# Graph convolution over 412,500 edges: six block buffers, scatters from chunk 369 on paced one by one, the second quad of nodes later

## Chip, cores and metric

The kernel runs on one core of one Trainium2 chip. The metric is the device time of one execution in microseconds; each version is timed several times and the median is compared. The engines are named as in the profile: PE is TensorE, DVE VectorE, ACT ScalarE, POOL GpSimd, SP SyncE.

## The reference

A graph convolution with a layer norm ahead of it and a residual around it. 12,500 nodes have 128 features each, 412,500 edges have 20 attributes and a weight each.

```python
h = relu(layernorm(x))                      # 12500 x 128
h = h @ W_in2f
Wij = ssp(f_ij @ W_f1 + b_f1) @ W_f2 + b_f2 # 412500 x 128, ssp(x) = softplus(x) - log 2
Wij = Wij * rcut_ij[:, None]
x_ij = h[idx_j] * Wij
agg = segment_sum(x_ij, idx_i, 12500)
return x + ssp(agg @ W_o1 + b_o1) @ W_o2 + b_o2
```

In the call `idx_i` is `src` and `idx_j` is `dst`; the edges come sorted by `dst`. So the rows `h[idx_j]` of neighbouring edges lie close together, and the sums over `idx_i` go to nodes all over the table.

## The kernel before

**Chunks and segments.** The edges are cut into 806 chunks of 512 (four tiles of 128). The chunks form seven segments; the first has chunks 0 to 351. Each chunk's 512 messages are computed and written, by four indirect DMAs (scatters) of 128 rows each, into slots of a table in HBM that are sorted by blocks of 128 target nodes. When a segment's last chunk is 17 steps back (`DELAY`), its collection begins: the slots of one block after another are read back (`m`), compared with the node numbers (`to`, L932), and added up by TensorE as products with the comparison (L953, into `acc`); `keep` (L987 on DVE for later segments) adds the result to the sums `agg`. So from step 369 (352 + 17) on a step holds a chunk's own work and a piece of collecting, called its units.

**A step.** The program is unrolled, and each engine executes its instructions in the order in which they are written. The function `step(k)` writes: the message of chunk `k` on DVE (`message`: the place L863, and `o = v * hg` L864); the end of the last rank on DVE (`rank_end`: `top` L771); on ACT the scaled rows of chunk `k+1` (`picked`: `hg`, L856); on PE the filters of chunk `k+1` (`value`: `v`, L834); on PE the picks of node rows of chunk `k+2` (`pick`, L846), from rows `near` that SP loaded; on ACT the bias of its `v` (L826); on DVE `at` (`window`, L818), every second step `r` (`hidden_end`, L742), and `inb`, which marks the block of each edge for a later chunk (`blocks`, L747); the comparisons `to` of the units; on PE the ranks of a later chunk (`pass_on` L799 and `rank` L766, which read `inb`), from which `top` and, for every four chunks, the slot numbers are made; every second step on ACT the softplus parts `a` (L719 to L722) and on PE the hidden layer `z` (`hidden`, L710); and last on PE the additions of the units (`add`, L953).

**The scatters.** `message` puts its chunk on the list `waiting`. The four scatters of a chunk (L873, on GpSimd's own DMA queue) read `o`, of which there are 16 buffers. The first 24 chunks scatter as soon as `o` is there. From chunk 24 (`PACED`) on, the scatters of chunk `k-1` (`LAG` is 1) are written right behind PE's `v` of chunk `k+1`, and the first of the four waits for the last matmul of that `v`; the other three follow with no wait for PE. In the last 12 steps nothing is paced. GpSimd does hardly anything else than scatters.

**The head.** The node table is made in quads of 512 nodes by `make_h`, a generator that does one stage at each call: statistics on DVE (L346, L347), normalisation on DVE (L355 to L362), transposition on PE (L367) and `relu` on ACT, the product with `W_in2f` on PE (L373), the split into three bf16 parts on ACT and DVE (L377, L380), and the writes of the table by SP (L386, L395). Quad 0 is made ahead of the loop. Quad 1 (`h[1]`) does its first stage in step 0 and one stage more at the end of each step from 0 on. `HEAD` (steps 0, 2, 4) places the hidden layer's parts in the first steps.

Of the kernel before, what the change touches and what calls it, by code (L numbers as in the profile page):

```python
# [11 lines left out]
F16 = mybir.dt.float16  # L12
# [33 lines left out]
def gnn_kernel(  # L46
# [498 lines left out]
    with tc.tile_pool(name="edge", bufs=2) as edge, tc.tile_pool(  # L545
# [57 lines left out]
        class Group:  # L603
# [101 lines left out]
            def hidden(self, c):  # L705

                z = psum.tile([P, 2, CH], F32, name="z")
                for k in range(2):
# [3 lines left out]
                    if k == 1:  # L712
                        behind(mm, self.g * NCHUNK + c - LZ, 3)
                self.pair[c] = z
# [30 lines left out]
            def blocks(self, c):  # L745
                inb = quad.tile([P, QT, NBLK], F16, name="inb")
# [6 lines left out]
            def rank(self, c):  # L753
# [8 lines left out]
                if k == seg.cleared and k > seg.c0:  # L762
# [3 lines left out]
                nc.tensor.matmul(free, after, self.inb[c], start=k == seg.c0, stop=False,  # L766
                                 skip_group_check=True)
# [61 lines left out]
            def value(self, c, v):  # L829
# [8 lines left out]
                kept["v"] = mm  # L838
                return v

            def pick(self, c, at, ps):
# [3 lines left out]
                for i in range(QT):  # L845
                    mm = nc.tensor.matmul(ps[:, i, :], at[:, i * P:(i + 1) * P], near,  # L846
                                          start=i == 0, stop=i == QT - 1, skip_group_check=True)
                    if i == 1:
                        behind(mm, k, 2 + k % 2)

# [16 lines left out]
            def scatter(self, c, after=None):  # L867

                views = self.seg.views
                o = self.o.pop(c)  # L870
                for i in range(QT):
# [8 lines left out]
                    if i == 0 and after is not None:  # L880
# [13 lines left out]
        class Collect:  # L894
# [47 lines left out]
            def add(self, u):  # L942
                b0, nb, t0, nt = self.units[u]
                m, to = self.m.pop(u), self.to.pop(u)
                for j in range(nb * nt):
# [5 lines left out]
                    if i == 0 and t == 0:  # L951
                        self.acc[b // few] = self.room(b // few)
                    nc.tensor.matmul(self.acc[b // few][:, i, :], m[:, j, :P], to[:, j, :],  # L953
                                     start=t == 0, stop=t == self.seg.tiles(b) - 1)
# [96 lines left out]
        LAG, PACED = 1, 24  # L1051

        def step(k, units=()):
# [12 lines left out]
            def message(k):  # L1066
                g, c = of(k)
                g.message(c, vs.pop(k), hgs.pop(k))
                waiting.append(k)
                scatter(k)  # L1070

            def scatter(k, after=None):
                while waiting and (waiting[0] < PACED or k >= NCH - PACED // 2
                                   or after is not None and waiting[0] <= k - LAG):
                    j = waiting.pop(0)
                    g, c = of(j)
                    g.scatter(c, after if j >= PACED and k < NCH - PACED // 2 else None)
# [3 lines left out]
            if not k:  # L1081
                next(h[1])
# [11 lines left out]
            if has(k + 1):  # L1094
                g, c = of(k + 1)
                hgs[k + 1] = g.picked(c, ps.pop(k + 1))
                if k + 1 not in vs:
                    vs[k + 1] = g.value(c, bs.pop(k + 1))
                    scatter(k, kept["v"])
            if k in HEAD:  # L1100
                part("log", k + LZ - 1, pairs(hidden_log))
            if has(k + 2):
# [3 lines left out]
                g.pick(c, ats.pop(k + 2), ps[k + 2])  # L1106
                if k + 2 > 0:
                    bs[k + 2] = g.bias(c)
            part("window", k + 3, window)
# [9 lines left out]
            if 0 <= k < HEAD[-1]:  # L1119
# [7 lines left out]
            for r in ready[-1:]:  # L1127
                next(r, None)
                tops.append(r)
            if k in HEAD:  # L1130
# [5 lines left out]
            for c, u in units:  # L1136
                if summed:
                    summed[0].add(summed[1])
                summed[:] = c, u

# [131 lines left out]
        with tc.manual_schedule():  # L1272
# [36 lines left out]
            for k in range(-3, max(NCH, max(units) + 1)):  # L1309
# [11 lines left out]
                if k >= 0:  # L1321
                    for m in h:
# [127 lines left out]
```

## Time and profile before

| | us |
|---|---|
| median of 3 runs | 5023.69 |
| their lowest and highest | 5019.35, 5025.19 |
| profiled execution | 5066.41 |
| its span, first to last instruction | 5064.7 |

The mean granted clock of TensorE in the profiled execution is 0.784 of full speed. Over the span PE is busy 71%, DVE 62%, POOL 62%, ACT 55%. Times in the quoted lines are microseconds unless marked ns; a line such as "L873 POOL" is an instruction written at line 873 of the kernel and executed by GpSimd. A group's row gives the number of instructions, their busy time and the mean of one in ns, and the idle time of the engine just before them with what ended most of it. "issue" is a gap in which the engine waited for nothing that the profile shows; "remote" is something that the trace could not name.

### The profile page before, as it was taken

How to read it: one execution, taken by the hardware profiler on the slowest of the kernel's cores; microseconds unless marked ns; L12 is line 12 of the kernel's file. 1: busy time of each engine (PE TensorE's matmuls, PEld its weight loads, DVE VectorE, ACT ScalarE, POOL GpSimd, SP SyncE). 2: the span in 40 equal slices, each digit the busy share in tenths (PEclk: the TensorE clock that was granted, in tenths of full speed). 3: DMA queues.
4: the chain of work that ended last, by engine and by line, in shares of the span. 5: the costliest groups of instructions: out<-in, count | busy, mean ns of one | idle time of the engine just before them, and what ended most of it. 6: DMA issues, size and time to landing. Idle time of an engine off the chain costs nothing. (4 is left out here: it accounts for less than half of the span.)

```text
span 5064.7 us, 68387 instructions
## 1 busy us (share of the span) xinstructions
PE 3601.4 (71%) x21594; PEld 2760.7 (55%) x21594; DVE 3149.0 (62%) x7192; ACT 2793.9 (55%) x5494; POOL 3135.5 (62%) x3298
## 2 busy tenths in 40 slices
PE   5666666566655565567777887887777787787778
PEld 3444444344433344356666666666666666666667
DVE  5565555555544454556666666666666676677767
ACT  5556566565555555555555555555555555555533
POOL 5566666666666666666666666666656666666553
PEclk7666666766666666679999888888988888888889
DMA  4555545445433334446657655567656765665658
GB/s 140 171 160 164 171 138 174 147 134 160 130 99 114 113 113 141 131 154 199 190 189 238 187 178 185 175 192 230 188 169 185 219 207 168 183 216 163 186 144 229
DMA packets 494767, 858.10 MB, mean 169 GB/s; under 512 B 141018, under 2 KB 276558, under 8 KB 494398
## 3 DMA queue, kind: packets, MB, share of 16 engines
q1 hardware_dynamic: 390798, 640.38, 42.3%
q0 software_dynamic: 103168, 213.15, 12.5%
q8 instruction: 174, 2.85, 0.2%
q14 instruction: 195, 1.60, 0.1%
q10 hardware_dynamic: 432, 0.13, 0.0%
HBM read 457.62 MB, written 395.69 MB: 168 GB/s over the span
## 5 line engine op out<-in xcount | busy, mean ns | idle before, releaser
L873 POOL DMA_INDIRECT slots<-o,slot x3224 | 3090.8, 959 | 1831.2 <-issue 808.9
L856 ACT ACTIVATE hg<-picked,rcut 128x128 f32<-128x128 f32 x3224 | 913.3, 366 | 1243.5 <-remote 356.7
L834 PEld LDWEIGHTS v<-wf,r 128*128 128x128 f32 x6448 | 1067.2, 247 | 324.2 <-issue 214.8
L834 PE MATMUL v<-wf,r 128*128 128x128 f32 x6448 | 1153.8, 335 | 73.4 <-issue 36.5
L864 DVE TENSOR_TENSOR o<-v,hg 128x512 f32<-128x512 f32 x806 | 553.0, 686 | 698.4 <-remote 207.0
L953 PEld LDWEIGHTS acc<-to,m 128*128 128x128 f32 x5660 | 782.1, 219 | 281.0 <-issue 144.0
L953 PE MATMUL acc<-to,m 128*128 128x128 f32 x5660 | 836.6, 308 | 117.1 <-DVE agg L987 45.2
L710 PE MATMUL z<-f,wf 20*128 20x512 f32 x1612 | 605.7, 826 | 355.7 <-issue 185.6
L771 DVE TENSOR_REDUCE top<-free 128x4 f32<-128x392 f32 x806 | 449.1, 557 | 602.2 <-remote 341.9
L932 DVE TENSOR_TENSOR to<-numbers,m 128x640 f32<-128x640 f32 (+3 forms) x793 | 630.4, 825 | 40.0 <-remote 12.0
L719 ACT ACTIVATE a<-z,bf 128x1024 f32<-128x1024 f32 x402 | 445.7, 1109 | 379.4 <-PE v L834 113.6
L747 DVE TENSOR_TENSOR inb<-numbers,blk 128x392 f16<-128x392 f32 x806 | 447.7, 556 | 297.3 <-PE picked L846 73.9
L846 PE MATMUL picked<-near,at 126*128 126x128 bf16 x3224 | 393.6, 248 | 330.2 <-issue 193.5
L799 PE MATMUL free<-inb,rest_of 128*128 128x392 f16 x806 | 318.1, 395 | 420.9 <-issue 277.2
L742 DVE SCALAR_TENSOR_TENSOR r<-z,nbf,a 128x1024 f32<-128x1024 f32 x402 | 513.5, 1277 | 127.9 <-ACT a L722 64.0
L826 ACT ACTIVATE v<-bf 128x512 f32<-128x512 f32 x806 | 486.6, 604 | 180.7 <-DVE o L864 72.5
L846 PEld LDWEIGHTS <-at 126*128 126x128 bf16 x3224 | 302.7, 114 | 389.7 <-issue 364.5
L953 PE MATMUL numbers<-to,m 128*128 128x128 f32 x2492 | 398.7, 324 | 121.0 <-DVE to L932 87.6
L953 PEld LDWEIGHTS numbers<-to,m 128*128 128x128 f32 x2492 | 367.5, 233 | 213.6 <-DVE to L932 136.6
L722 ACT ACTIVATE a<-a,half 128x1024 f32<-128x1024 f32 x402 | 461.5, 1148 | 13.1
L710 PEld LDWEIGHTS z<-f,wf 20*128 20x128 f32 x1612 | 152.4, 226 | 551.7 <-issue 303.0
L720 ACT ACTIVATE a<-a 128x1024 f32<-128x1024 f32 x402 | 424.9, 1057 | 12.8
(126 smaller groups left out, 1845.0 us busy)
## 6 DMA issues: line engine op xcount, KB each, us to landing
m<-slots SPq DMA_DIRECT2D x307, 387.0 KB
rel<-rel_d SPq DMA_DIRECT2D x202, 504.0 KB
m<-slots SPq DMA_DIRECT2D x278, 322.5 KB
f<-in_f_t SPq DMA_DIRECT2D x101, 512.0 KB
slots<-o,slot POOLq DMA_INDIRECT x3224
m<-slots SPq DMA_DIRECT2D x193, 258.0 KB
slots<-zero SPq DMA_DIRECT2D x96, 387.0 KB
slots<-zero SPq DMA_DIRECT2D x58, 516.0 KB
```

What stands on the lines that cost most here:

```text
L710: mm = nc.tensor.matmul(z[:, k, :], wf1[rows, :], self.f[rows, :], start=True, stop=True)
L722: nc.scalar.activation(a, a, AF.Ln, bias=half, scale=0.5)
L742: nc.vector.scalar_tensor_tensor(r, z, nbf1, a, op0=ALU.max, op1=ALU.add)
L771: nc.vector.tensor_reduce(self.top[:, c * QT:(c + 1) * QT], free_v, axis=mybir.AxisListType.X, op=ALU.max)
L826: nc.scalar.activation(v, spread(bf12, QT), AF.Copy)
L834: mm = nc.tensor.matmul(v[:, i, :], r[:, i * P:(i + 1) * P], wf2, start=False, stop=True, skip_group_check=True)
L846: mm = nc.tensor.matmul(ps[:, i, :], at[:, i * P:(i + 1) * P], near, start=i == 0, stop=i == QT - 1, skip_group_check=True)
L856: nc.scalar.activation(hg[:, i, :], ps[:, i, :], AF.Copy, scale=self.rcut[:, j:j + 1])
L864: nc.vector.tensor_mul(o[:, :, :P], v, hg)
L873: put = nc.gpsimd.indirect_dma_start(out=views[j % VIEWS], out_offset=bass.IndirectOffsetOnAxis(ap=self.slot[:, j:j + 1], axis=0), in_=o[: ...
L932: nc.vector.tensor_tensor(to[:, :n, :], count_ps[:, None, :].to_broadcast([P, n, P]), m[:, :n, P:].to_broadcast([P, n, P]), op=ALU.is_equal)
L953: nc.tensor.matmul(self.acc[b // few][:, i, :], m[:, j, :P], to[:, j, :], start=t == 0, stop=t == self.seg.tiles(b) - 1)
```

## The change

It has three parts.

- `inb` has six buffers of its own in place of the pool's three.
- From chunk 369 on (`LONE`, the first segment's end plus `DELAY`) the four scatters of chunk `k-1` are written one at a time, at four points of step `k`: behind `v`, behind the picks, behind the rank, and at the end of the step behind its additions or its `z`. Each waits for PE's last matmul so far (`kept["mm"]`). Chunks 24 to 368 go as before.
- Quad 1 does its stages after steps 6 and later in place of steps 0 to 5; in steps 1 and 3 the hidden layer's `z` and the `v` of chunk `k+2` are written right behind the picks, and the message of chunk 5 is written at the end of step 4.

```diff
--- before.py
+++ after.py
@@ -711,6 +711,7 @@
                                           start=True, stop=True)
                     if k == 1:
                         behind(mm, self.g * NCHUNK + c - LZ, 3)
+                kept["mm"] = mm
                 self.pair[c] = z
 
             def hidden_log(self, c):
@@ -743,7 +744,7 @@
                 self.pair[c] = r
 
             def blocks(self, c):
-                inb = quad.tile([P, QT, NBLK], F16, name="inb")
+                inb = quad.tile([P, QT, NBLK], F16, name="inb", bufs=6)
                 nc.vector.tensor_tensor(
                     inb, count_ps[:, None, :NBLK].to_broadcast([P, QT, NBLK]),
                     self.blk[:, c * QT:(c + 1) * QT, None].to_broadcast([P, QT, NBLK]),
@@ -763,8 +764,8 @@
                     used = self.used()
                     self.limit(6 * len(segs), ALU.is_gt, seg.low, used[:, :, :NBLK - 1])
                     self.limit(6 * len(segs) + 1, ALU.is_gt, seg.low_last, used[:, :, NBLK - 1:])
-                nc.tensor.matmul(free, after, self.inb[c], start=k == seg.c0, stop=False,
-                                 skip_group_check=True)
+                kept["mm"] = nc.tensor.matmul(free, after, self.inb[c], start=k == seg.c0,
+                                              stop=False, skip_group_check=True)
                 kept["inb"] = self.inb[c]
 
             def rank_end(self, c):
@@ -835,7 +836,7 @@
                                           start=False, stop=True, skip_group_check=True)
                     if i == 1:
                         behind(mm, k, k % 2)
-                kept["v"] = mm
+                kept["mm"] = mm
                 return v
 
             def pick(self, c, at, ps):
@@ -847,6 +848,7 @@
                                           start=i == 0, stop=i == QT - 1, skip_group_check=True)
                     if i == 1:
                         behind(mm, k, 2 + k % 2)
+                kept["mm"] = mm
 
             def picked(self, c, ps):
 
@@ -864,11 +866,11 @@
                 nc.vector.tensor_mul(o[:, :, :P], v, hg)
                 self.o[c] = o
 
-            def scatter(self, c, after=None):
+            def scatter(self, c, tiles, after=None):
 
                 views = self.seg.views
-                o = self.o.pop(c)
-                for i in range(QT):
+                o = self.o[c] if tiles[-1] < QT - 1 else self.o.pop(c)
+                for i in tiles:
                     j = c * QT + i
                     put = nc.gpsimd.indirect_dma_start(
                         out=views[j % VIEWS],
@@ -877,7 +879,7 @@
                         in_offset=None,
                     )
                     puts.append(put.ins.name)
-                    if i == 0 and after is not None:
+                    if i == tiles[0] and after is not None:
                         tc.add_manual_dep(
                             put.ins, after.ins.name,
                             mybir.DependencyInfo(mybir.DependencyClass.Sync,
@@ -950,8 +952,9 @@
                     i = b % few
                     if i == 0 and t == 0:
                         self.acc[b // few] = self.room(b // few)
-                    nc.tensor.matmul(self.acc[b // few][:, i, :], m[:, j, :P], to[:, j, :],
-                                     start=t == 0, stop=t == self.seg.tiles(b) - 1)
+                    kept["mm"] = nc.tensor.matmul(
+                        self.acc[b // few][:, i, :], m[:, j, :P], to[:, j, :],
+                        start=t == 0, stop=t == self.seg.tiles(b) - 1)
                     if t == self.seg.tiles(b) - 1 and (i == few - 1 or b == NBLK - 1):
                         self.done.append((b, few))
                         owed.append(self)
@@ -1049,6 +1052,7 @@
         tops, ps = [], {}
         waiting = []
         LAG, PACED = 1, 24
+        LONE = segs[0].c1 + DELAY
 
         def step(k, units=()):
 
@@ -1066,20 +1070,34 @@
             def message(k):
                 g, c = of(k)
                 g.message(c, vs.pop(k), hgs.pop(k))
-                waiting.append(k)
+                waiting.append((k, 0))
                 scatter(k)
 
-            def scatter(k, after=None):
-                while waiting and (waiting[0] < PACED or k >= NCH - PACED // 2
-                                   or after is not None and waiting[0] <= k - LAG):
-                    j = waiting.pop(0)
-                    g, c = of(j)
-                    g.scatter(c, after if j >= PACED and k < NCH - PACED // 2 else None)
+            def scatter(k, point=None):
+                while waiting:
+                    j, i = waiting[0]
+                    if j < PACED or k >= NCH - PACED // 2:
+                        n, after = QT - i, None
+                    else:
+                        where, n = ("v", QT) if j < LONE else ("each", 1)
+                        if point not in (("v", "pick", "rank", "end") if where == "each" else (where,)):
+                            return
+                        if j * QT + i + n > (k - LAG + 1) * QT:
+                            return
+                        after = kept["mm"]
+                    while n > 0:
+                        j, i = waiting.pop(0)
+                        g, c = of(j)
+                        e = min(QT, i + n)
+                        g.scatter(c, range(i, e), after)
+                        after = None
+                        n -= e - i
+                    if e < QT:
+                        waiting.insert(0, (j, e))
+                        return
 
             if k in vs:
                 message(k)
-            if not k:
-                next(h[1])
             for r in tops:
                 for _ in r:
                     pass
@@ -1096,7 +1114,7 @@
                 hgs[k + 1] = g.picked(c, ps.pop(k + 1))
                 if k + 1 not in vs:
                     vs[k + 1] = g.value(c, bs.pop(k + 1))
-                    scatter(k, kept["v"])
+                    scatter(k, "v")
             if k in HEAD:
                 part("log", k + LZ - 1, pairs(hidden_log))
             if has(k + 2):
@@ -1104,8 +1122,12 @@
                 if k + 2 not in ps:
                     ps[k + 2] = psum.tile([P, QT, P], F32, name="picked", tag="v", bufs=3)
                 g.pick(c, ats.pop(k + 2), ps[k + 2])
+                scatter(k, "pick")
                 if k + 2 > 0:
                     bs[k + 2] = g.bias(c)
+                if k in (1, 3):
+                    part("hidden", k + LZ, pairs(hidden))
+                    vs[k + 2] = g.value(c, bs.pop(k + 2))
             part("window", k + 3, window)
             if k not in HEAD:
                 part("end", min(k + LZ - 2, made.get("log", -1)), pairs(hidden_end))
@@ -1116,7 +1138,7 @@
                     keep()
             if k < NCH:
                 keep()
-            if 0 <= k < HEAD[-1]:
+            if 0 <= k <= HEAD[-1]:
                 message(k + 1)
             upto = max(made["rank"], min(k + LR, 2 * k + 3))
             ready = [ranks(j) for j in range(made["rank"] + 1, upto + 1)]
@@ -1127,6 +1149,7 @@
             for r in ready[-1:]:
                 next(r, None)
                 tops.append(r)
+            scatter(k, "rank")
             if k in HEAD:
                 part("end", made["log"] - 1, pairs(hidden_end))
             elif k != -1:
@@ -1137,6 +1160,7 @@
                 if summed:
                     summed[0].add(summed[1])
                 summed[:] = c, u
+            scatter(k, "end")
 
         zeros = {}
         units = {}
@@ -1319,7 +1343,7 @@
                 step(k, now)
 
                 if k >= 0:
-                    for m in h:
+                    for m in h[:1] if k <= HEAD[-1] + 1 else h:
                         next(m, None)
                 if k > NEXT - 3:
                     next(aside, None)
```

**GpSimd**, scatters of two chunks in the second half of the program (`slots1` is the second segment's table, `o` a chunk's messages; DMASW are the scatters' own queue lanes, and the number behind a name in the wait is a count that is left open). Before:

```order
L873 DMA slots1_117<-o_19231,slot_18948 116992x129 [waits DMASW0_49,DVE_49,PE_49]
L873 DMA slots1_117<-o_19231,slot_18948 116992x129 [waits DMASW1_49]
L873 DMA slots1_117<-o_19231,slot_18948 116992x129 [waits DMASW2_49]
L873 DMA slots1_117<-o_19231,slot_18948 116992x129 [waits DMASW3_49]
L873 DMA slots1_117<-o_19284,slot_18948 116992x129 [waits DMASW4_49,DVE_49,PE_49]
L873 DMA slots1_117<-o_19284,slot_18948 116992x129 [waits DMASW5_49]
L873 DMA slots1_117<-o_19284,slot_18948 116992x129 [waits DMASW6_49]
L873 DMA slots1_117<-o_19284,slot_18948 116992x129 [waits DMASW7_49]
```

After, the same scatters:

```order
L875 DMA slots1_117<-o_19231,slot_18946 116992x129 [waits DMASW0_49,DVE_49,PE_49]
L875 DMA slots1_117<-o_19231,slot_18946 116992x129 [waits DMASW1_49,PE_49]
L875 DMA slots1_117<-o_19231,slot_18946 116992x129 [waits DMASW2_49,PE_49]
L875 DMA slots1_117<-o_19231,slot_18946 116992x129 [waits DMASW3_49,PE_49]
L875 DMA slots1_117<-o_19284,slot_18946 116992x129 [waits DMASW4_49,DVE_49,PE_49]
L875 DMA slots1_117<-o_19284,slot_18946 116992x129 [waits DMASW5_49,PE_49]
L875 DMA slots1_117<-o_19284,slot_18946 116992x129 [waits DMASW6_49,PE_49]
L875 DMA slots1_117<-o_19284,slot_18946 116992x129 [waits DMASW7_49,PE_49]
```

The scatters stand in the same order. The second, third and fourth of each chunk now wait for PE too.

**PE in the head**, from the picks of chunk 3 to those of chunk 4 (`z` the hidden layer, `xps` the transposition of quad 1, `v_461` before and `v_438` after the filters of chunk 3). Before:

```order
L846 MATMUL picked_456<-near_285,at_405 128x128
L799 LDWEIGHTS rest_of_78
L799 MATMUL free_144<-inb_409,rest_of_78 128x392
L766 LDWEIGHTS after_77
L766 MATMUL free_144<-inb_465,after_77 128x392
L799 LDWEIGHTS rest_of_78
L799 MATMUL free_144<-inb_465,rest_of_78 128x392
L766 LDWEIGHTS after_77
L766 MATMUL free_144<-inb_467,after_77 128x392
L710 MATMUL z_483<-f_227,wf1_62 128x512 x2
L367 MATMUL xps_486<-ident_58,xb_236 128x128 x4
L834 MATMUL v_461<-wf2_63,r_426 128x128 x4
```

After:

```order
L847 MATMUL picked_433<-near_285,at_392 128x128
L710 MATMUL z_440<-f_227,wf1_62 128x512 x2
L835 MATMUL v_438<-wf2_63,r_413 128x128 x4
L800 LDWEIGHTS rest_of_78
L800 MATMUL free_144<-inb_396,rest_of_78 128x392
L767 LDWEIGHTS after_77
L767 MATMUL free_144<-inb_449,after_77 128x392
L800 LDWEIGHTS rest_of_78
L800 MATMUL free_144<-inb_449,rest_of_78 128x392
L767 LDWEIGHTS after_77
L767 MATMUL free_144<-inb_451,after_77 128x392
L847 LDWEIGHTS at_447
```

`z` and `v` of chunk 3 now stand right behind the picks of chunk 3, ahead of four rank products, and quad 1's transposition is gone from between them.

**SP in the head**: `h3_1` to `h3_3` and `h3` are the node tables, `near` the loads of node rows from them. Before:

```order
L629 DMA rel_592<-rel_d_114 126x2048
L386 DMA h3_1_89<-hb_543 128x3x384
L386 DMA h3_2_90<-hb_543 128x4x384
L386 DMA h3_3_91<-hb_543 128x2x384
L395 DMA h3_87<-hb_543 128x4x384
L649 TENSOR_LOAD shift0_130
L656 ISA
L656 DMA near_692<-h3_1_89 126x128
L656 ISA
L656 DMA near_694<-h3_1_89 126x128
```

After, from the third of those loads on:

```order
L629 DMA rel_752<-rel_d_114 126x2048
L656 ISA
L656 DMA near_754<-h3_1_89 126x128
L1335 DMA slots0_116<-zero_82 96x1032 x2
L656 ISA
L656 DMA near_841<-h3_1_89 126x128
L386 DMA h3_1_89<-hb_838 128x3x384
L386 DMA h3_2_90<-hb_838 128x4x384
L386 DMA h3_3_91<-hb_838 128x2x384
L395 DMA h3_87<-hb_838 128x4x384
```

The four writes of quad 1, which stood ahead of four loads from `h3_1`, stand behind them; those loads read rows of quad 0 alone.

## The prediction

> **What bounds the kernel now.** I read the page first, for the engine that is busy longest on work that can't be shared out; then the windows before and after the collection of segments begins, for the time of one chunk in each; then the waits of GpSimd; then a timeline inside the part that the change touches.
>
> ```profile
> span 5064.7 us, 68387 instructions
> PE 3601.4 (71%) x21594; PEld 2760.7 (55%) x21594; DVE 3149.0 (62%) x7192; ACT 2793.9 (55%) x5494; POOL 3135.5 (62%) x3298
> L873 POOL DMA_INDIRECT slots<-o,slot x3224 | 3090.8, 959 | 1831.2 <-issue 808.9
> ```
>
> No engine is full. GpSimd is 62% busy, but each of its 3224 scatters also leaves a fixed gap (808.9 us called "issue"), so that its floor is higher than its busy time tells. Counting the `o` of DVE (L864, one for each chunk) in three windows from the start gives the pace (window, its length, busy time of those instructions and their count, granted clock, share of the DMA engines, GB/s):
>
> ```profile
> 0.00:200.00 200.00, 19.88 (x29) 0.71 0.49 151
> 0.00:2200.00 2200.00, 252.88 (x368) 0.66 0.46 142
> 0.00:4800.00 4800.00, 541.37 (x789) 0.78 0.54 168
> ```
>
> From 200 to 2200 us 368 - 29 = 339 chunks pass, 5.90 us each. From 2200 to 4800 us, which begins almost exactly at chunk 369, it is 789 - 368 = 421 chunks, 2600/421 = 6.18 us each. The second part has TensorE's additions (L953) in every step, and it is the part that the change paces anew. GpSimd there (start, duration, and in brackets the idle time before it and what ended it):
>
> ```profile
> 3603.28 0.95 POOL L873 DMA_INDIRECT slots<-o,slot  x1 [1.84 <-PE z L710]
> ...
> 3607.07 0.96 POOL L873 DMA_INDIRECT slots<-o,slot  x1 [0.30 <-issue]
> 3609.26 0.95 POOL L873 DMA_INDIRECT slots<-o,slot  x1 [1.24 <-PE acc L953]
> ...
> 3618.10 0.96 POOL L873 DMA_INDIRECT slots<-o,slot  x1 [0.30 <-issue]
> 3621.30 0.96 POOL L873 DMA_INDIRECT slots<-o,slot  x1 [2.25 <-PE free L766]
> ...
> 3625.09 0.95 POOL L873 DMA_INDIRECT slots<-o,slot  x1 [0.30 <-issue]
> 3627.38 0.95 POOL L873 DMA_INDIRECT slots<-o,slot  x1 [1.34 <-PE free L766]
> ...
> 3633.41 0.96 POOL L873 DMA_INDIRECT slots<-o,slot  x1 [1.29 <-PE acc L953]
> ```
>
> Inside a run the scatters follow each other by (3618.10 - 3609.26)/7 = 1.263 us, so four cost at least 5.05 us. This window holds runs of 4, 8, 4 and 4, each followed by a stop of 1.24 to 2.25 us; five chunks take 30.13 us, 6.03 each. What the stop waits for is seen on the other engines in the same window:
>
> ```profile
> 3608.72 1.06 PE L834 MATMUL v<-wf,r 128*128 128x128 f32 x8
> 3613.49 2.27 PE L953 MATMUL acc<-to,m 128*128 128x128 f32 x18
> 3619.30 0.22 PE L846 MATMUL picked<-near,at 126*128 126x128 bf16 x1 [1.20 <-issue]
> 3616.48 1.14 ACT L856 ACTIVATE hg<-picked,rcut 128x128 f32<-128x128 f32 x4 [5.62 <-PE acc L953]
> 3617.19 0.57 DVE L771 TENSOR_REDUCE top<-free 128x4 f32<-128x392 f32 x1 [2.34 <-PE v L834]
> ```
>
> During the run of 8 (to 3619.06) TensorE does its work, but ACT stands 5.62 us and DVE 2.34 us for results of TensorE, and then TensorE itself does its picks one by one, 1.2 us apart. An earlier place shows it in the extreme:
>
> ```profile
> 1008.46 0.96 POOL L873 DMA_INDIRECT slots<-o,slot  x1 [0.30 <-issue]
> 1011.21 1.14 ACT L856 ACTIVATE hg<-picked,rcut 128x128 f32<-128x128 f32 x4 [9.66 <-remote]
> 1012.35 0.96 POOL L873 DMA_INDIRECT slots<-o,slot  x1 [2.93 <-remote]
> ```
>
> ACT waits 9.66 us, and its wait ends only 1.8 us after the run's last scatter does (1009.42). I read this so: while scatters follow each other without a stop, news of TensorE's progress reaches the other engines late, and it gets through after GpSimd stops. The kernel is bound by this loop, 5.05 us of scatters and then a stop until the news is through, not by an engine's work.
>
> **The new pace of the scatters, from chunk 369 on.** It holds to chunk 792 (later chunks go unpaced, before and after), 424 chunks. No scatter is added or moved among the scatters; the first of four keeps its wait for `v`; the second, third and fourth wait for the picks, the rank and the last matmul of that same step. That is three more waits for each chunk, 1272. The waiting itself costs GpSimd an instruction each:
>
> ```profile
> L873 POOL DMA_INDIRECT slots<-o,slot x3224: 952/958/1177, 23.2 to 4924.9; - x190
> L873 POOLq EVENT_SEMAPHORE  x832: 17/43/8809, 30.1 to 4912.1; - x167
> ```
>
> With a median of 43 ns (the three numbers are least, median, most) it fits in the 0.30 us between two scatters, so I take 0 (if it did not, 1272 x 43 ns = 55 us, the upper bound). Behind a waiting scatter on GpSimd stands only the next scatter; who waits for scatters is the collection seventeen chunks later, and `o`'s buffers, sixteen chunks deep, so neither is near. What decides is whether the wait is open when a scatter comes to it. In the window above, the fourth scatter of the second chunk of the run of 8 starts at 3618.10, and the last addition of its step ends at 3615.76, 2.3 us before: by the records open. But the stops show that the news may come later than the records, and so some of the fourth scatters will stop.
>
> What does a stop in a new place cost? The stop after a run of 8 is 2.25 us, less the 0.30 that would be there anyway 1.95 for two chunks; those after runs of 4 are 1.24, 1.34 and 1.29, less 0.30 about 1.0 for one. So the price goes with the length of the run, some 0.25 us a scatter. If that holds for shorter runs too, a stop before the fourth scatter shortens the next one by as much, and the move costs nothing; that is the value I take. The other bound is a stop that costs 1.24 - 0.30 = 0.94 however short the run: 424 x 0.94 = 400 us if every chunk had one more. I take the first because two lengths of run show it and none shows the second.
>
> And what can be won? The mean chunk takes 6.18 us, the undisturbed ones above 6.03. The difference, 0.15 x 424 = 64 us, is in long irregular waits (GpSimd's, in total, times, longest):
>
> ```profile
> POOL slots L873 <- PE free L766: 162.1, 84, 2.8
> POOL slots L873 <- PE picked L846: 112.9, 43, 5.5
> POOL slots L873 <- PE z L710: 47.4, 36, 2.2
> ```
>
> From 2400 to 4400 us, 43 waits that end on a pick take 2.63 us each, up to 5.5, twice the 1.32 of those that end on `z`: 43 x 1.31 = 56 us, and over the 2620 us of 424 chunks 74. They come when a run has gone on so long that the picks themselves are late, as at 3619.30. With a wait in each quarter GpSimd can no longer be eight scatters ahead on one piece of news, and what it stops for is nearer, so ACT, DVE and the picks get theirs before the next chunk's first scatter. Some of these stops, those after a run of 8 at 2.25, pay for two chunks and are no loss. So I take 0.11 of the 0.15 us: 424 x 0.11 = 47 us off, between 0 and 74.
>
> The Trainium skill (Perfetto Trace Analysis, "Summary: the profiler window per engine type") says that the end recorded for a TensorE instruction is an estimate and that the travel of its semaphore is hidden. By that rule the 2.3 us of lead above need not be a lead; the trace agrees where ACT waits 5.62 us. It leaves the sum at -47 if stops only move, and turns it into the slower rival below if they add up.
>
> **Six buffers for the blocks.** In the order of instructions DVE's L747 loses only waits on DVE itself; its 155 waits on PE are the same, as they come from the PSUM tile it reads. The row that could bear a buffer's wait is this one, of what L747 idled for:
>
> ```profile
>   PE free L766: 64.2, 18
> ```
>
> If all 18 were the reader of an old block it would be 64 us of DVE, which does not bound; but they are of the late kind above. Gain taken 0, bounds -64 and 0; the buffers themselves add no instruction.
>
> **The second quad of nodes later.** The normalisation, transposition, product and four stores of quad 1 leave the steps 0 to 5 and come after step 6; two pairs of `z` and `v` move up behind the picks.
>
> ```profile
> 35.60 0.96 POOL L873 DMA_INDIRECT slots<-o,slot  x1 [2.38 <-DVE o L864]
> 42.50 0.96 POOL L873 DMA_INDIRECT slots<-o,slot  x1 [2.16 <-DVE o L864]
> 49.23 0.95 POOL L873 DMA_INDIRECT slots<-o,slot  x1 [1.99 <-DVE o L864]
> 57.83 0.96 POOL L873 DMA_INDIRECT slots<-o,slot  x1 [3.86 <-DVE o L864]
> 41.53 0.69 DVE L864 TENSOR_TENSOR o<-v,hg 128x512 f32<-128x512 f32 x1 [2.98 <-PE v L834]
> 38.60 1.12 PE L367 MATMUL xps<-ident,xb 128*128 128x128 f32 x4
> 39.51 1.91 PE L834 MATMUL v<-wf,r 128*128 128x128 f32 x8
> ```
>
> Here alone GpSimd waits for `o`: 10.39 us in four waits, 9.2 beyond the regular 0.30. One of them waits on `v`, which stood behind quad 1's transposition of 1.12 us; that alone is 1 us, all four 9.2. After the move the same work falls where GpSimd has chunks in stock, and SP's four stores stand behind four loads of nodes that read quad 0 only. If they were late for the loads behind them, the 1.12 us and its like come back once: I bound the loss by the same 9.2, and take the middle of the gain, -5.
>
> **Sum.** 5064.7 - 47 + 0 - 5 = 5012.7 us of span. The profiled execution took 5066.41 us, 1.7 beyond its span, and 42.7 more than the median of the runs, 5023.69. So 5012.7 + 1.7 - 42.7 = **4972 us**, 1.0% less.
>
> **Rivals.** *Stops add up (slower).* The place is the fourth scatter: it waits for the additions, which end the step, and `v` of the next step follows directly, so GpSimd may stop twice in a chunk. If each stop has a price of its own, 0.94 us, the 47 us are eaten when more than 47/0.94 = 50 of the 424 chunks have an extra stop, 1 in 8. With 1 in 3 it is 141 x 0.94 = 133 us, less 52: 5105 us. For it speaks how late ACT hears of TensorE; against it that the price of a stop went with the run's length.
>
> *Nothing moves.* All waits are open when GpSimd comes to them, so the change does not pace at all there; runs of 8 stay, and only the head's 5 us remain: 5019 us. For it speaks the lead of 2.3 us; against it the late picks.
>
> *Runs of 8 disappear and the news is in time.* Then the step falls to the pace that the first part reaches with the same scatters, 5.90 us: 424 x 0.28 = 119 us, with the head 4900 us. TensorE would allow it:
>
> ```profile
> 2200.00:4800.00 2600.00, 2053.72 (x13834) 1672.31 (x13834) 1775.36 (x3761) 1414.72 (x2786) 1613.67 (x1685) 0.87 0.62 191
> ```
>
> it is busy 2053.72/421 = 4.88 us a chunk, DVE 4.22. Against it: the two parts differ in additions and in the clock, and a faster pace needs stops shorter than any in the timeline.
>
> **Chances.** The forecast 0.45; stops add up 0.27; nothing moves 0.13; the larger gain 0.15. Two runs of this kernel can be told apart from about 0.2%, 10 us. Faster: the forecast except its weakest edge, and the larger gain, 0.59; same: nothing moves and that edge, 0.14; slower: 0.27. The forecast's own range is 4942 (-74 and -9) to 5020 (no gain but 4 of the head). To leave out no more than 2 in 10 I go down to 4895, just beyond the larger gain, and up to 5095, which takes in extra stops in up to about 3 chunks of 10.
>
> **What would show it.** Right: from 2200 to 4800 us about 428 chunks (2600/6.07); in the timeline stops before the fourth scatter, and the stop before the first one shorter by as much; waits that end on picks down from 43 and none of 5 us; ACT's waits for `hg` below 5 us; scatters still near 958 ns. For the head: the first 60 us without waits for `o` of 2 us and more. Wrong: more than one stop in most chunks with a sum over 1.13 us (6.18 - 5.05), or the same runs of 4 and 8 as before. If the L766 waits of L747 go but the pace stays, the buffers were worth nothing; if the time falls with the scatters' pattern unchanged, they were worth what I gave to the pace.

## The result and the profile after

The changed kernel takes 5000.72 us in the median of 5 runs (4992.46 to 5005.22), the kernel before 5023.69 us (5019.35 to 5032.8) beside it: a ratio of 0.9952, 95% interval 0.9937 to 0.9967. The forecast was 4972 us, 52 us less than before; the runs show 23 less. The direction is right, the size less than half.

In the profile of the changed kernel, the page's row of the scatters and the count of `o` from 2200 to 4800 us (window, length, busy time and count, clock, DMA share, GB/s):

```profile
span 4990.7 us, 69636 instructions
L875 POOL DMA_INDIRECT slots<-o,slot x3224 | 3101.1, 962 | 1740.1 <-issue 772.5
2200.00:4800.00 2600.00, 293.07 (x427) 0.88 0.64 194
```

427 chunks in place of 421, almost the 428 forecast. That agreement is luck, and this is the trap of this case: the two profiles differ by 74 us of span where the medians differ by 23. Chunks 30 to 368, which the pace does not touch, also passed faster, at 5.84 us each in place of 5.90. The profile of before (5066.41 us) lay 43 us above its median, and in three later jobs (each a set of kernels timed together on one chip) the kernel before had medians of 5066.62, 5070.75 and 5073.23 us. So one job's profile can't be held against another's for 1%, and what follows compares kernels of one job, by ratios to the kernel before in that same job.

In three more jobs the kernel before took 4202 to 4209 us in place of 5024 to 5073, on one and the same chip 4209 in one job and 5073 in the next, and nothing in between was seen; what differs in the traces is told with the experiments.

### The profile page after: what moved, and what is told of

Read it like the earlier page. It is cut to its first block, busy times and chain, and to the rows that moved or that the text cites. A ratio compares the mean times of both kernels' runs of the same rounds, so it can differ in the third digit from the quotient of the medians.

```text
span 4990.7 us, 69636 instructions
## 1 busy us (share of the span) xinstructions
PE 3578.4 (72%) x21594; PEld 2746.7 (55%) x21594; DVE 3151.6 (63%) x7192; ACT 2788.5 (56%) x5494; POOL 3145.9 (63%) x3298
## 5 line engine op out<-in xcount | busy, mean ns | idle before, releaser
L875 POOL DMA_INDIRECT slots<-o,slot x3224 | 3101.1, 962 | 1740.1 <-issue 772.5
L955 PEld LDWEIGHTS acc<-to,m 128*128 128x128 f32 x5660 | 778.4, 218 | 280.2 <-issue 171.7
L955 PE MATMUL acc<-to,m 128*128 128x128 f32 x5660 | 831.2, 307 | 119.5 <-issue 56.8
L934 DVE TENSOR_TENSOR to<-numbers,m 128x640 f32<-128x640 f32 (+3 forms) x793 | 630.3, 825 | 35.7 <-remote 16.5
L955 PE MATMUL numbers<-to,m 128*128 128x128 f32 x2492 | 397.2, 324 | 125.8 <-DVE to L934 65.4
L955 PEld LDWEIGHTS numbers<-to,m 128*128 128x128 f32 x2492 | 367.4, 233 | 213.6 <-DVE to L934 110.1
```

What stands on the lines that cost most here:

```text
L875: put = nc.gpsimd.indirect_dma_start(out=views[j % VIEWS], out_offset=bass.IndirectOffsetOnAxis(ap=self.slot[:, j:j + 1], axis=0), in_=o[: ...
L934: nc.vector.tensor_tensor(to[:, :n, :], count_ps[:, None, :].to_broadcast([P, n, P]), m[:, :n, P:].to_broadcast([P, n, P]), op=ALU.is_equal)
L955: kept["mm"] = nc.tensor.matmul(self.acc[b // few][:, i, :], m[:, j, :P], to[:, j, :], start=t == 0, stop=t == self.seg.tiles(b) - 1)
```

## The experiments

**Each part alone, and the kernel before again.** Four kernels of one job. The pace without the buffers and the head:

```diff
-                inb = quad.tile([P, QT, NBLK], F16, name="inb", bufs=6)
+                inb = quad.tile([P, QT, NBLK], F16, name="inb")
...
-                if k in (1, 3):
-                    part("hidden", k + LZ, pairs(hidden))
-                    vs[k + 2] = g.value(c, bs.pop(k + 2))
...
-                    for m in h[:1] if k <= HEAD[-1] + 1 else h:
+                    for m in h:
```

> The kernel before with the new pace of the scatters alone (three block buffers, quad 1 in its old place). The whole change took 23 us off the median (5023.69 to 5000.72). Theory A, the pace is what gains: 4998 to 5008 us, and from chunk 369 to 792 the profile shows about 6.06 us a chunk, as in the changed kernel. Theory B, the pace is worth nothing and the gain lies in the head and the buffers: 5018 to 5028 us, with a chunk at the pace of the kernel before. Theory C, the pace costs and the rest hides it: over 5030 us.

Measured 0.9957 (0.9942 to 0.9972). Theory A: the pace alone carries the change. (Its times of 4998 to 5008 us do not apply, as the kernel before took 5066.62 us in this job, and its 6.06 us a chunk did not come: by the starts of the scatters a chunk from 369 to 792 takes 6.14 us, where the kernel before of this job has 6.16.) The head alone, the same lines of the change put into the kernel before:

> The kernel before with quad 1 moved later alone. As predicted, 5 us off: 5014 to 5021 us, chunk 30 scattered 5 to 10 us earlier than in the kernel before. Rival from the two profiles, where the four waits of 10.4 us in the head became two of 9.2: nothing off, 5020 to 5028 us. Rival that the head carries the change: under 5010 us.

Measured 1.0001 (0.9988 to 1.0015): nothing. In its timeline of GpSimd, what is left of the four waits for `o` in the head:

```profile
44.59 0.96 POOL L873 DMA_INDIRECT slots<-o,slot  x1 [6.36 <-DVE o L864]
57.48 0.96 POOL L873 DMA_INDIRECT slots<-o,slot  x1 [3.00 <-DVE o L864]
```

Two waits of 9.36 us together in place of four of 10.39. The scatters of chunk 2 start 2.2 us sooner (33.5 us in place of 35.7 in this job's kernel before), and then GpSimd is out of messages for longer; chunk 30 starts at 215.2 us, not earlier than the 213.3 of the kernel before. The buffers alone:

```diff
-                inb = quad.tile([P, QT, NBLK], F16, name="inb")
+                inb = quad.tile([P, QT, NBLK], F16, name="inb", bufs=6)
```

> The kernel before with six buffers for the blocks alone. As predicted nothing: 5019 to 5028 us and the same runs of scatters. Rival: the profile of the changed kernel also gained 20 us between chunks 30 and 368, where the pace is unchanged; if the buffers did that, 5000 to 5010 us and an earlier chunk 368.

Measured 1.0011 (0.9997 to 1.0025): nothing. The control:

> The kernel before, word for word, for a second profile and as a measure of the noise. Its first profiled execution took 5066 us, 43 above the median. If that lay in the execution: a profile near 5024 us, and the time from chunk 30 to 368 within 10 us of the changed kernel's 1972 us. If the profile itself costs 40 us: near 5066 again. Ratio 1.000 within 0.002.

Measured 0.9993 (0.9978 to 1.0008), a profile of 5047.22 us where this job's runs of the kernel before had a median of 5066.62 (5050.94 to 5083.19). So the profile does not cost 40 us; single executions spread, and the jobs differ. From chunk 30 to 368 it took 1989 us, 17 more than the changed kernel's 1972 and not within 10: what the changed kernel's profile gained there belongs to its job and not to the change.

Within this job the two profiles may be compared stretch by stretch; not by their spans, which are single executions (5045.5 us, and 5054.2 for the pace alone, the other way than the medians). First the count of `o` from 2200 to 4800 us, of the kernel before (first row) and in the next fence of the pace alone:

```profile
2200.00:4800.00 2600.00, 288.96 (x421) 0.88 0.63 193
```

```profile
2200.00:4800.00 2600.00, 291.64 (x424) 0.88 0.63 193
```

Three chunks more. Then the waits of GpSimd from 2400 to 4400 us (total, times, longest), the kernel before:

```profile
POOL slots L873 <- PE free L766: 140.6, 70, 2.9
POOL slots L873 <- PE picked L846: 105.1, 42, 6.2
POOL slots L873 <- remote: 75.6, 44, 2.7
POOL slots L873 <- PE z L710: 49.1, 35, 2.2
POOL slots L873 <- PE acc L953: 17.0, 13, 2.0
...
POOL slots L873 <- PE numbers L953: 9.2, 7, 1.3
```

and the pace alone:

```profile
POOL slots L875 <- PE acc L955: 109.3, 80, 7.6
POOL slots L875 <- remote: 79.4, 61, 2.2
POOL slots L875 <- PE numbers L955: 59.3, 42, 6.5
POOL slots L875 <- PE free L767: 57.6, 47, 2.6
POOL slots L875 <- PE z L710: 48.6, 41, 2.0
POOL slots L875 <- PE picked L847: 47.5, 35, 2.2
```

The waits that end on the rank and the picks fall from 245.7 to 105.1 us, as forecast, and the long ones on a pick are gone (6.2 to 2.2). But 142.4 us more (109.3 + 59.3 - 17.0 - 9.2) now end on the additions, L953 before and L955 here, and among them are waits of 7.6 and 6.5 us. So this view, which sorts waits by the name of what ended them, does not tell what was won: a wait that leaves one row can stand in another. The names are uncertain too, since in these jobs the traces hold only part of the semaphore updates from which they are inferred (3458 of TensorE's 4063 in this kernel before, 3004 of DVE's 6529). In the timeline of the pace alone GpSimd makes runs of 3, 4, 4, 5 and 4 there:

```profile
3599.81 0.96 POOL L875 DMA_INDIRECT slots<-o,slot  x1 [1.02 <-PE acc L955]
...
3604.60 0.96 POOL L875 DMA_INDIRECT slots<-o,slot  x1 [1.30 <-remote]
...
3610.65 0.96 POOL L875 DMA_INDIRECT slots<-o,slot  x1 [1.30 <-PE acc L955]
...
3616.73 0.96 POOL L875 DMA_INDIRECT slots<-o,slot  x1 [1.32 <-PE free L767]
...
3624.27 0.96 POOL L875 DMA_INDIRECT slots<-o,slot  x1 [1.52 <-remote]
...
3630.31 0.96 POOL L875 DMA_INDIRECT slots<-o,slot  x1 [1.29 <-PE acc L955]
```

From the starts of all scatters of the chunks 369 to 792 in the traces comes this table: ahead of which scatter of a chunk GpSimd stops (a distance of over 1.45 us from the scatter before), in what share of the chunks, and how much that is over 1.265 us, as a mean over all chunks (the control and the pace alone, of one job; then, told of below, the fourth scatter alone at the end of the step, two orders without that end, and the four points from chunk 24 on, of a second job; and the short fill, of a third):

```
                 1st          2nd          3rd          4th         stops   us in all
before_again  0.69 1.10    0.00 0.00    0.00 0.00    0.00 0.00       293     467
pace_only     0.30 0.32    0.10 0.09    0.01 0.01    0.44 0.65       361     451
fourth_at_end 0.27 0.29    0.00 0.00    0.00 0.00    0.51 0.79       328     451
no_end        0.68 1.05    0.06 0.05    0.00 0.00    0.00 0.00       312     465
two_and_two   0.69 1.08    0.00 0.00    0.04 0.04    0.00 0.00       307     472
each_from_24  0.28 0.29    0.08 0.07    0.01 0.01    0.49 0.71       363     456
pad_each_3    0.60 0.88    0.01 0.09    0.02 0.09    0.01 0.09       269     361
```

With a quarter more stops (293 to 361) the stopped time falls by 16 us of 467. (In the last row the four means of 0.09 and a part of 0.88 are the fills told of below.)

Two things move against each other in this sum. All lengths of stops here are what goes over the 1.265 us. In the kernel before (control) a stop lasts 1.02 us in the median after a run of four scatters and 1.87 after a run of eight. In the pace alone it lasts 0.89 after a run of one, 1.27 after two, 0.83 after three, 1.01 after four and 1.82 after eight; runs shorter than four, of which there were none, are now 78 of the 361. Take each stop at the median for its length as the usual part, and what it lasts beyond as the irregular part. In the three kernels of this job with the old pace (head, buffers, control) the usual part is 407 to 410 us and the irregular part 57 to 61; in the pace alone they are 431 and 20. The irregular part falls by 37 to 41 us, the usual part rises by 21 to 25. Stops of over 2.5 us fall from 19 to 22 (71 to 81 us) to 5 (30 us), but the longest, of 8.3 us, is no shorter than the 7.8 of the control.

**Which of the four points does it.** The function that lets scatters go, with a point for each of the four in a list:

```diff
-                        where, n = ("v", QT) if j < LONE else ("each", 1)
-                        if point not in (("v", "pick", "rank", "end") if where == "each" else (where,)):
+                        at = ("v",) * QT if j < LONE else POINTS
+                        if point != at[i]:
                             return
+                        n = at[i:].count(at[i])
...
+        POINTS = ("v", "v", "v", "end")
```

> The kernel before with a new pace in which, from chunk 369 on, the first three scatters of a chunk go behind v as before and only the fourth waits, for the end of the step. With all four points the ratio was 0.9957. Theory A, the fourth scatter's wait is the only one that closes often (in that run a stop of more than 0.2 us stood before 44% of the fourth scatters, 10% of the second, 1% of the third), so it carries the change: 0.994 to 0.997. Theory B, each quarter counts: 0.997 to 1.000.

Measured 0.9965 (0.9952 to 0.9978), and the table's row is close to that of all four points: theory A. With `POINTS = ("v", "pick", "rank", "rank")`:

> The same with the fourth scatter let go with the third, at the rank: points v, picks, rank, rank. Theory A: without the wait for the end of the step the stops stay before the first scatter, and the ratio is 0.999 to 1.001. Theory B: the picks and the rank do part of it, 0.996 to 0.999.

Measured 1.0001 (0.9986 to 1.0017), again A. With `POINTS = ("v", "v", "rank", "rank")`:

> The same with the first two scatters at v and the last two at the rank. Theory A: as without the end, 0.999 to 1.001. Theory B: halves of a chunk give half of the gain or more, 0.996 to 0.998.

Measured 0.9994 (0.9982 to 1.0006), A. The picks and the rank are mostly open when a scatter comes to them (the table has stops before 4 to 10% of the scatters that wait there); only the end of the step closes often. And with the four points of the change from chunk 24 on (`LONE = PACED`):

> The quarters from chunk 24 on, where GpSimd now makes runs of 12. If the idle time only goes with the number of scatters, wherever the stops are, the first part keeps its 5.90 us a chunk and the ratio is that of the change, 0.994 to 0.998. If each stop has a price of its own, one stop more in every chunk of 344 at some 0.5 us costs 170 us: 1.02 to 1.05.

Measured 0.9950 (0.9936 to 0.9964): the idle time does not rise with the stops. In chunks 30 to 368 it made 197 stops where the kernel before of the other job had 147, and 274.9 us in all where that had 279.7 (the other three kernels of its own job, with the old pace there: 150 to 153 stops, 283 to 294 us). More stops do not add up here, and the first part neither gains nor loses more than the noise.

**Fills in GpSimd's time.** If the stopped time is time in which TensorE's news has to get through, it should take other work of GpSimd for nothing. Into the kernel before, behind each scatter of chunks 369 to 792 (a spare tile, so the output is the same):

```diff
                     puts.append(put.ins.name)
+                    if 369 <= self.g * NCHUNK + c <= 792:
+                        nc.gpsimd.memset(pad, 0.0)
```

and, in another, two longer fills behind the fourth scatter alone. The first try of both, with two kernels on the places:

> The same with one short fill (128 x 128 floats, 0.20 us where the trace has one) behind each of the four scatters, so that the 1.07 us of idle time a chunk would be spread over four gaps. Theory N: the news trickles through in the gaps and the stop shrinks by their sum, 0.99 to 1.01. Theory B: 424 x 4 x 0.2 = 340 us more, 1.05 to 1.08.

> The kernel before with two fills of a spare tile on GpSimd (128 x 512 floats each, about 1.06 us together by the fill of 128 x 1032 that took 0.96 us) behind the fourth scatter of each chunk from 369 to 792; nothing else is changed. Theory N, a stop is the time in which TensorE's news get through, and it gets through whenever no scatter is being made: the fills lie in the stop, which shrinks by as much, and the time is nearly the same, ratio 0.995 to 1.02. Theory B, GpSimd's own work sets the pace and the stop comes on top: 424 x 1.06 = 450 us more, 1.07 to 1.10.

> The kernel before with all four scatters of a chunk, from 369 on, at the end of the step in place of v. The fourth scatter alone at the end gave 0.9965. Theory P, the place matters (the stop then lies where TensorE starts on v and the picks): 0.994 to 0.998. Theory S, it is the split of the chunk that breaks the runs of 8: with one stop a chunk again nothing is gained, 0.999 to 1.003.

> The changed kernel with the quarters from chunk 24 on. The pace alone gave 0.9957 from chunk 369 and 0.9950 from chunk 24, so if the parts add up 0.994 to 0.997, no better than the change beyond the noise. A version that beats both would be under 0.993.

Measured 1.0344 (1.0329 to 1.0360), 1.1078 (1.1061 to 1.1094), 1.0002 (0.9993 to 1.0011) and 0.9996 (0.9987 to 1.0005), beside a kernel before of 4202.1 us. This tests none of the theories: in this job GpSimd does not stop at all from chunk 369 to 792, so that fills cost their full price, 0.344 us a chunk for the short ones, and no wait for TensorE has anything to close. The second try, with the change itself:

> The short fill behind each scatter once more (0.344 us a chunk on the chip without stops). If this chip has the stops (kernel before near 5060 us): Theory N, the news gets through whenever no scatter is being made, so the fills come out of the stops, 0.99 to 1.01; Theory B, stop and fills add up, 424 x 0.344 = 146 us, 1.025 to 1.035. On a chip without stops (before near 4200 us): 1.034 again.

> The two fills behind the fourth scatter once more (1.07 us a chunk on the chip without stops). With stops: Theory N 0.995 to 1.02, Theory B 424 x 1.07 = 454 us, 1.08 to 1.10. Without stops: 1.108 again.

> All four scatters at the end of the step once more. With stops: Theory P, the end of the step is the better place for the one stop, 0.994 to 0.998; Theory S, only the split of the chunk gains, 0.999 to 1.003. Without stops: 1.000.

> The changed kernel, word for word. With stops: 0.994 to 0.997, as in its first comparison. Without stops: 0.999 to 1.001, since GpSimd makes scatters without a break there and no wait closes; this says whether the gain belongs to the chip.

Measured 1.0345 (1.0331 to 1.0359), 1.1076 (1.1060 to 1.1091), 0.9998 (0.9989 to 1.0007) and 0.9993 (0.9984 to 1.0002), beside 4208.88 us: without stops again, and there the change is worth nothing. Its profile, the scatters' row and the timeline of GpSimd:

```profile
L875 POOL DMA_INDIRECT slots<-o,slot x3224 | 3103.3, 963 | 1005.2 <-issue 572.4
```

```profile
2999.26 0.96 POOL L875 DMA_INDIRECT slots<-o,slot  x1 [0.30 <-PE picked L847]
3000.53 0.96 POOL L875 DMA_INDIRECT slots<-o,slot  x1 [0.30 <-PE numbers L955]
...
3011.92 0.96 POOL L875 DMA_INDIRECT slots<-o,slot  x1 [0.30 <-issue]
```

A scatter takes what it took, 963 ns, and the distance is 1.266 us ((3011.92 - 2999.26)/10); but the idle time is 1005.2 us, 0.31 a scatter, where it was 1740.1, and ACT's longest wait for `hg` in that stretch is 1.58 us. So the news that comes late in the other jobs is in time here, with the same program. (The names behind the arrows say little here; all waits are the regular 0.30.)

The short fill once more, now in a job with stops, on the chip of the second:

> The short fill behind each scatter a third time, for a chip with stops (before near 5060 us): Theory N 0.99 to 1.01, Theory B 1.025 to 1.035. Without stops 1.034, as twice before.

Measured 1.0014 (0.9996 to 1.0032) beside 5073.23 us, in place of the 1.0345 that the fills cost without stops: theory N. GpSimd in it:

```profile
3601.29 0.96 POOL L874 DMA_INDIRECT slots<-o,slot  x1 [0.16 <-issue]
3602.24 0.22 POOL L882 MEMSET pad<- 128x128 f32 x1
...
3603.98 0.96 POOL L874 DMA_INDIRECT slots<-o,slot  x1 [0.16 <-issue]
3604.94 0.22 POOL L882 MEMSET pad<- 128x128 f32 x1
3606.61 0.96 POOL L874 DMA_INDIRECT slots<-o,slot  x1 [1.45 <-remote]
```

Of the 146 us that the fills cost without stops 7 remain by the ratio, between none and 16. In the traces a stop after a run of 8 falls from 2.01 us in the mean (over the regular distance, control) to 1.42 here, by 0.59 where two chunks' fills are 0.69; the control is of another job.

**Is the news late, or TensorE itself?** The traces hold the times at which semaphores were updated, so the two can be held against each other. In the control, chunks 369 to 792, GpSimd's stops are 21% of the time, and 21% of the TensorE instructions that update its semaphore end in them. But 60% of the updates recorded (1262 of 2090) fall in them, over four a stop, where one would end it. For DVE it is 10% of the ends and 11% of the updates, for ACT 14 and 18%. The records are not complete (2090 updates for 2369 such instructions, and under half for DVE and ACT); if all that are missing for TensorE lay outside the stops, its share would still be 53%. So TensorE's work ends at all times alike, and by the records its news comes mainly while GpSimd stops.

**Place or split.** What all four scatters at the end of the step give where the stops occur, the two jobs without stops could not tell. Once more:

> All four scatters at the end of the step a third time. Where the stops occur (before near 5060 us): Theory P, the end of the step is the better place for the one stop, 0.994 to 0.998; Theory S, only the split of the chunk gains, 0.999 to 1.003. Without stops (before near 4200 us) 1.000, as twice before.

Measured 0.9997 (0.9988 to 1.0006) beside 4202.18 us, without stops a third time. Whether the 0.4% comes from the end of the step as a place, or from splitting the chunk into three and one, stays open.

## Why the prediction came out as it did

- **What bounds the kernel**: right for the jobs with stops. A chunk costs four scatters, 5.06 us, and about 1.1 us in which the news gets through; the fills, which cost 146 us without stops and 7 with them (0.0014 of 5073), show that this time goes to no work of GpSimd. That it is no engine's work the jobs without stops show: 5.06 us a chunk, with the same program. That TensorE's news comes late, which I had read from a few waits, the recorded updates bear out (60% of them in 21% of the time).
- **The stop's price: here the step failed.** I put it at nothing: a stop before the fourth scatter "shortens the next one by as much", at 0.25 us a scatter, measured on runs of four and eight. For shorter runs this does not hold: after one, two and three scatters a stop lasts 0.89, 1.27 and 0.83 us, not 0.25 to 0.75. So the usual part of the stops rose by 21 to 25 us, on a term that stood at 0. The other bound, 0.94 us however short the run, is near for these short runs; it did not make the kernel slower because it was not paid on top: the stops after runs of eight fell from 128 to 22.
- **What is won**, 47 us: the irregular part of the stops fell by 37 to 41 us, near it, and the 64 us that I gave the whole of it is near its 57 to 61; the upper bound of 74 was too wide. What I gave as the reason came only in part. The long waits that ended on picks vanished (6.2 to 2.2 us), but waits of 7.6 us ended on the additions, and ACT did not get its news sooner: from chunk 369 to 792 its waits of over 5 us for `hg`, of which I forecast none, rose from 15 in the control to 37. Why the irregular part falls stays open.
- **The two together**: 16 to 18 us off in the profiles of one job, and by the ratio of the pace alone 0.43% of 5023.69, 22 us (14 to 29), 0.05 us a chunk in place of 0.11. The division into two parts was made after the fact, from one profile of each kernel.
- **Each quarter**: I let all three new waits count. Picks and rank seldom close, and without the end of the step nothing is won (1.0001 and 0.9994); the fourth alone gives 0.9965, its interval overlapping that of all four.
- **The head**, -5: measured 0 (1.0001, 0.9988 to 1.0015). The term summed waits one by one, though all four end on the same thing, GpSimd being ahead of the messages. With quad 1's work moved away GpSimd waits once for 6.36 us in place of 2.38, 2.16 and 1.99, so the sign that I named, no wait for `o` of 2 us and more in the first 60 us, did not come.
- **The buffers**, 0: right (1.0011, 0.9997 to 1.0025).
- **Rivals.** Stops that add up: there are 68 more stops, but their sum is smaller, so it falls. Nothing moves: true without stops (0.9993). The larger gain, news in time: its pace of 5.90 was no floor, since without stops it is 5.06, but no change of pace brings it about. The Trainium skill (Perfetto Trace Analysis, "Summary: the profiler window per engine type") says that the travel of a TensorE instruction's semaphore is hidden from its record. The runs agree: the wait of the fourth scatter, by the records open 2.3 us before in the one place that I looked at, closed in 44% of the chunks.

No kernel tried beats the change beyond the noise: the quarters from chunk 24 on gave 0.9950 without buffers and head, the change 0.9952, each in a job of its own.

## What to carry to other kernels

Before a gain is booked for moving a wait, add up all the time that the engine waits, before and after, by the length of the run of work ahead of it: a row of the view of waits can empty because its waits took another name, and what long waits give back, new short ones can take. A price measured on two lengths of run need not hold for a shorter one. Whether a stop is only waiting can be tested by filling it with idle work of the same engine. And a term of 1% is not read from two profiles of different jobs; put the control, and a profile of it, into each job.

## What the runs showed of the hardware

The same program ran in two conditions, with medians of the kernel before of 5024 to 5073 us and of 4202 to 4209, one chip showing both. The scatters take GpSimd 0.96 us and a distance of 1.265 us in either. What differs is how soon other engines go on after TensorE: from chunk 369 to 792 of the changed kernel ACT waits for `hg` for over 5 us 25 times in the one and 3 times in the other. In the one, in the control, 60% of TensorE's recorded semaphore updates fall in GpSimd's stops, 21% of the time; in the other there are no such stops. The granted clock differs as well, 0.781 to 0.794 for the kernel before in the one and 0.834 to 0.847 in the other; but a matmul of `v` takes 333 ns and 323 ns in the changed kernel's two profiles, 3%, where the time differs by 20%. What sets the condition no run here shows.
